# One gate block of a filtered feed-forward layer moved from VectorE to ScalarE and GpSimd, and the order of the sums around it

## The chip, the cores and the metric

The kernel runs on one core of a Trainium2 chip. A core has five engines with a queue of their own each: TensorE (PE, matrix products; its weight loads are shown as PEld), VectorE (DVE), ScalarE (ACT), GpSimd (POOL) and SyncE (SP, which here issues the DMAs). Each queue runs in the order in which it was written, and an instruction that waits holds up everything behind it on its engine. The metric is the device time of one execution in microseconds (us), the median over several runs.

## The reference

Four layers follow each other on an image x of 2 batches, 64 channels and 256 x 256 points, each of the form x = x + layer(group_norm(x)). Layer 0 is a weighted sum over neighbours, layer 1 two state-space scans over the points, layer 3 a rounded cosine transform. The change is in layer 2:

```python
def _L2_conv_ref(x, w_in, w_dw, fft_filter, w_out):
    x = jnp.einsum('bchw,oc->bohw', x, w_in)          # 64 -> 384 channels
    B, C, H, W = x.shape
    xp = x.reshape(B, C, H // p, p, W // p, p).transpose(0, 1, 2, 4, 3, 5)
    xf = jnp.fft.rfft2(xp) * fft_filter               # on patches of 8 x 8
    xp = jnp.fft.irfft2(xf, s=(p, p))
    x = xp.transpose(0, 1, 2, 4, 3, 5).reshape(B, C, H, W)
    x = lax.conv_general_dilated(x, w_dw, window_strides=(1, 1),
            padding=[(1, 1), (1, 1)], feature_group_count=C)   # 3 x 3, by channel
    x1, x2 = jnp.split(x, 2, axis=1)                  # 192 gates, 192 values
    x = jax.nn.gelu(x1, approximate=False) * x2
    return jnp.einsum('bchw,oc->bohw', x, w_out)      # 192 -> 64 channels
```

So each point of 192 channels needs nine multiply-adds for its gate, nine for its value, a gelu of the gate and a product of the two.

## The kernel before

**Tiles.** All data is float32. The 2 x 64 channels of the input stand on 128 partitions. The 384 hidden channels of two batches are six blocks of 128 partitions: gates a0 and a1 (128 channels of batch 0 and of batch 1), a2 (the other 64 of both batches), and values b0, b1, b2 in the same way. The image is worked in 32 strips of 8 rows. A strip's six blocks lie in three tiles `z[s, p]` (two blocks each, 10 rows with the two rows kept from the strip before). The 3 x 3 filter works on halves of four rows, h = 0 and 1; the projection on quarters of two rows, e = 0 and 1.

**The front stage** makes a strip's z. For one tile of patches t: `norm` (ACT, L191, into xn2), `turn` (four transposes on PE, L897, into the PSUM bank po2, copied to xT by ACT, L899), `fourier` (products with the Fourier basis, L905, again into po2, copied to xf, L907). Then for each of its four groups `hidden` makes two products f (L915, two PSUM banks), `scaled` multiplies them with the filter on VectorE into gf (L922), and `image` brings them back to the image (L941, two PSUM banks pz), from where ACT copies them into z (L949).

**The filter stage** of a strip, with each block's 3 x 3 taps done by one of three means:
- on TensorE (`gate_pe`): nine products with a diagonal matrix, L1064, summed in the single PSUM bank pcv; ACT then takes the gelu into the tile gl (L1072). Blocks (h, a0) of both halves.
- on ACT and GpSimd (`gate_pool`): ACT makes the product with one tap (L1017, the first into gl, the others into one of three buffers `prod`), GpSimd adds it to gl (L1021), two rows at a time; the gelu is put off until the third tap of the next piece (`flush`, L995). Blocks (0, a1), (1, a2), (1, a1).
- on VectorE (`taps_of`): the first tap L977, eight more L980, in the PSUM tile acc (two banks, one buffer). `gate_dve` does so for the gate block (0, a2), with the last tap into gl and a gelu behind it; `value_dve` for all six value blocks, with the product of gate and value behind it (L1049).

**The end.** `project` makes the output of two rows (L1093, L1100) in po2, `finish` adds it to the input xr (L1111), takes the statistics for the next norm (L1112) and stores it. po2 has one buffer, which `turn`, `fourier` and `project` share: each has to wait until the one before was read.

**The order** is written out by hand (`tc.manual_schedule`): instructions stand on each engine in the order in which the program issues them, and the waits follow from the tiles. The loop runs over u, half a tile of the front stage; strip s is filtered nine steps later, v = u - 9, in eight steps of two parts g. I call these 16 parts of a strip its slots, i = 0 to 15 (slot i is step j = i // 2, part g = i % 2). A slot issues: the f of `hidden`, two of VectorE's list `dve`, the gf of `scaled`, the rest of VectorE's share (`quota` spreads the list evenly over 16 slots), a projection if one is due, then in an inner loop images, tap products of TensorE's list `pe` and steps of GpSimd's list `gps`, and then `finish` and `turn`. Outputs are due in slots 2 and 5 (the strip before, half 1) and in 10 and 13 (half 0). The boundary rows of the next strip (`edges`, GpSimd, L957 and L959) are copied in slot 14.

```python
dve = gate_dve(s, 0, 2)
for h in range(2):
    for i in ((2, 1, 0), (2, 0, 1))[h]:
        dve += value_dve(s, h, i)
```

Of the kernel before, what the change touches and what calls it, by code (L numbers as in the profile page):

```python
# [10 lines left out]
F32 = mybir.dt.float32  # L11
BF16 = mybir.dt.bfloat16
AF = mybir.ActivationFunctionType
ALU = mybir.AluOpType
# [3 lines left out]
P = 128  # L18
# [102 lines left out]
class Kernel:  # L121
# [695 lines left out]
    def layer2(self, x, y, coeffs):  # L817
        nc, tc, a = self.nc, self.tc, self.a
# [14 lines left out]
        nstrip = H // 8  # L833
        with ExitStack() as ctx:
# [47 lines left out]
                x_half[n] = t  # L882

            def norm(t):
                xn = pool.tile([P, 4, P], F32, name="xn2")
                at = slice(64 * (t % 2), 64 * (t % 2) + 64)
                self.affine(
                    xn.rearrange("p g (i c) -> p i g c", c=16),
                    x_half[t // 2][:, :, at].rearrange("p i (g c) -> p i g c", c=16),
                    coeffs,  # L890
                )
                x_n[t] = xn
# [9 lines left out]
            def fourier(t):  # L902
                pf = p_o.tile([P, 4, P], F32, name="po2")
                for g in range(4):
                    nc.tensor.matmul(pf[:, g], x_T[t][:, g], fwd, start=True, stop=True)  # L905
                xf = pool.tile([P, 4, P], F32, name="xf")
                nc.scalar.copy(xf, pf)  # L907
                x_f[t] = xf
# [75 lines left out]
                return [lambda k=k: step(k) for k in range(9)], box  # L984

            def new_gl(s, h, i, r):
                t = pool.tile([P, 4, W], F32, name="gl", bufs=6)
                gl[s, h, i] = t
                return t[:, :r]

            def new_acc(r):
                return p_a.tile([P, 4, W], F32, name="acc")[:, :r]
# [10 lines left out]
            def gate_pool(s, h, i, r=4):  # L1003

                name, out = f"a{i}", []

                def step(m, n, k):
                    if k == 2:
                        flush()
                    w = taps[name][:, k : k + 1]  # L1010
                    if m == k == 0:
                        new_gl(s, h, i, r)
                    acc = gl[s, h, i][:, m : m + n]
                    prod = acc
                    if k:
                        prod = pool.tile([P, 2, W], F32, name="prod", bufs=3)[:, :n]
                    nc.scalar.activation(  # L1017
                        prod, near(s, name, 4 * h + m, n, k), AF.Copy, scale=w
                    )
                    if k:  # L1020
                        nc.gpsimd.tensor_add(acc, acc, prod)  # L1021
                    if k == 8:
                        late.append(acc)

                for m in range(0, r, 2):
                    for k in range(9):
                        out.append(lambda m=m, k=k: step(m, min(2, r - m), k))
                return out

            def gate_dve(s, h, i, r=4):  # L1030
                ops, box = taps_of(
                    nc.vector,
                    s,
                    f"a{i}",
                    4 * h,
                    r,
                    lambda: new_acc(r),
                    lambda t: new_gl(s, h, i, r),
                )
                return ops[:8] + [lambda: (ops[8](), gelu(gl[s, h, i][:, :r]))]  # L1040

            def value_dve(s, h, i, r=4):
                ops, box = taps_of(
                    nc.vector, s, f"b{i}", 4 * h, r, lambda: new_acc(r), lambda t: t
                )

                def gate():
                    t = gl[s, h, i][:, :r]
                    nc.vector.tensor_tensor(t, t, box["t"], ALU.mult)  # L1049

                return ops + [gate]

            def gate_pe(s, h, i, r=4):
                out = []
# [61 lines left out]
            def quota(n, i, parts):  # L1116
                return n * (i + 1) // parts - n * i // parts

            E = mybir.EngineType
            with tc.manual_schedule(engines={E.PE, E.DVE, E.Activation, E.Pool, E.SP}):  # L1120
                frame(0)
                edges(0)
                load_half(0)
                load_half(1)
                norm(0)
                turn(0)
                fourier(0)
                n_u = 8 * nstrip
                dve, pe, gps = [], [], []
                for u in range(n_u + 12):  # L1130
                    t, odd = divmod(u, 2)
                    front = u < n_u
                    v = u - 9
                    s, j = divmod(v, 8)
                    if j == 0 and 0 <= s < nstrip:
                        dve = gate_dve(s, 0, 2)
                        for h in range(2):
                            for i in ((2, 1, 0), (2, 0, 1))[h]:
                                dve += value_dve(s, h, i)
                        pe = gate_pe(s, 0, 0) + gate_pe(s, 1, 0)  # L1140
                        gps = gate_pool(s, 0, 1) + gate_pool(s, 1, 2) + gate_pool(s, 1, 1)
                        n_dve, n_gps = len(dve), len(gps)
                    if front:
                        if u % 4 == 2 and u // 4 + 2 < 2 * nstrip:
                            load_half(u // 4 + 2)
                        if not odd and t + 1 < 4 * nstrip:
                            norm(t + 1)
                    if u % 8 == 1 and 0 < u - 1 < n_u:
                        frame(u // 8)

                    out = None
                    if 0 <= v:
                        hv, part = divmod(v - 4, 4)
                        if 0 <= hv < 2 * nstrip and part in (0, 1):
                            reload(*divmod(hv, 2), part)
                        hv, part = divmod(v - 5, 4)
                        if 0 <= hv < 2 * nstrip and part in (0, 1):
                            out = (*divmod(hv, 2), part)
                    for g in range(2):
                        i = 2 * j + g  # L1160
                        left = quota(n_dve, i, 16) if 0 <= v and dve else 0
                        if front:
                            ph = hidden(t, 2 * odd + g)
                        for _ in range(min(2, left)):
                            dve.pop(0)()
                        if front:
                            scaled(t, 2 * odd + g, ph)
                        for _ in range(left - min(2, left)):
                            dve.pop(0)()
                        if out and g == odd:  # L1170
                            po = project(*out)
                        images = ((0, 1), (2,))[g] if 0 < u <= n_u else ()
                        n_pe = min(3, len(pe))
                        for n in range(3):
                            if n < len(images):
                                image(u - 1, images[n])
                            if n < n_pe:
                                pe.pop(0)()
                            if i < 14 and 0 <= v and gps:
                                for _ in range(quota(n_gps, 3 * i + n, 42)):  # L1180
                                    gps.pop(0)()
                            if n == 1 and g == 0 and odd and front and t + 1 < 4 * nstrip:
                                fourier(t + 1)
                        if i == 14:
                            flush()
                            if 0 <= s < nstrip:
                                if s + 1 == nstrip:
                                    frame(nstrip)
                                edges(s + 1)
                        if out and g == 1:  # L1190
                            finish(*out, po)
                        if g == 1 and not odd and front and t + 1 < 4 * nstrip:
                            turn(t + 1)


                assert not (dve or pe or gps)
                s = nstrip
                reload(s, 0, 0)
                for op in gate_pool(s, 0, 1, 1) + gate_pe(s, 0, 0, 1) + gate_dve(s, 0, 2, 1):
                    op()  # L1200
                flush()
                for i in (2, 1, 0):
                    for op in value_dve(s, 0, i, 1):
                        op()
                finish(s, 0, 0, project(s, 0, 0))
# [109 lines left out]
```

## Time and profile before

| What | us |
|---|---|
| median of 3 runs (lowest, highest) | 19872.43 (19870.87, 19875.25) |
| the profiled execution, its own time | 19870.25 |
| its span, first to last instruction | 19868.5 |
| busy in the span: VectorE | 18868.2 (95%) |
| busy in the span: GpSimd | 15933.1 (80%) |
| busy in the span: TensorE | 14671.3 (74%) |
| busy in the span: ScalarE | 11805.5 (59%) |

The profile is of one execution. The busy shares are means over layers with different limits, so that what a change in layer 2 does has to be read from layer 2's part of the span. In a row of groups the columns are line, engine, operation, output and inputs with their shapes, count, busy time, mean ns of one, and the idle time of the engine just before them with what ended it. In a row of waits, "A <- B: x, n, m" says that A stood idle for x us in total until B, n times, m at most. A row of a stretch of time has the busy time of each engine in it and TensorE's granted share of its clock.

### The profile page before, as it was taken

To read this page: it belongs to the slowest core of one execution; us is meant where nothing else is said; L and a number is where in the kernel's file an instruction comes from. 1 tells how busy PE (TensorE), PEld (TensorE's weight loads), DVE (VectorE), ACT (ScalarE), POOL (GpSimd) and SP (SyncE) were. 2 spreads that over 40 slices of the span, in tenths; PEclk is the share of its full clock that TensorE was granted. 3 is DMA by queue.
4 is the path that set the end of the run, shared out by engine and by line. 5 is a ranking of instruction groups with operands and counts; after the bars stand their busy time and mean duration, and the time that the engine had idled before them with its cause. 6 is when DMAs were issued, how large, how long until landed. Compare 5 with 4: busy or idle time off the path is not lost. (4 is left out here: it accounts for less than half of the span.)

```text
span 19868.5 us, 162340 instructions
## 1 busy us (share of the span) xinstructions
PE 14671.3 (74%) x48720; PEld 4849.2 (24%) x48720; DVE 18868.2 (95%) x16476; ACT 11805.5 (59%) x16810; POOL 15933.1 (80%) x7816
## 2 busy tenths in 40 slices
PE   6886777677767767677677767677777688888886
PEld 3332111111111111111111111111111144444444
DVE  7998999999999999999999999999999989999997
ACT  1224666666666666666666666666666655555554
POOL 4776888888888888888888888888888855555554
PEclk9997666666666666666666666666666689989998
DMA  3114666666666666666666666666666500000003
GB/s 118 47 46 110 152 152 153 151 154 150 155 148 157 147 157 147 157 148 156 149 154 151 153 152 153 152 153 151 152 151 152 136 29 29 29 29 29 29 27 144
DMA packets 662179, 2438.82 MB, mean 123 GB/s; under 512 B 131888, under 2 KB 201264, under 8 KB 450160
## 3 DMA queue, kind: packets, MB, share of 16 engines
q1 hardware_dynamic: 661296, 2428.43, 50.9%
q8 instruction: 385, 6.31, 0.1%
q14 instruction: 498, 4.08, 0.1%
HBM read 1990.14 MB, written 437.78 MB: 122 GB/s over the span
## 5 line engine op out<-in xcount | busy, mean ns | idle before, releaser
L792 DVE TENSOR_TENSOR_SCAN h<-da,st,h 128x512 f32<-128x512 f32 x8192 | 9837.4, 1262 | 309.0 <-ACT da L789 223.8
L796 POOL TENSOR_TENSOR h<-h,cb 128x2048 f32<-128x2048 f32 x2048 | 9255.6, 4519 | 166.0 <-POOL st L795 1.5
L789 ACT ACTIVATE da<-dl,p_a 128x512 f32<-128x512 f32 x8192 | 5564.8, 688 | 3985.3 <-DVE h L792 3892.6
L561 PE MATMUL py<-h,t_c_quad 128*32 128x512 f32 x16384 | 3254.7, 817 | 1656.9 <-POOL h L796 1655.9
L561 PE MATMUL pb<-bc,t_c_sel 64*128 64x512 f32 x3072 | 2696.9, 972 | 2379.9 <-DVE h L773 2374.3
L773 DVE TENSOR_TENSOR h<-dv,pb 128x2048 f32<-128x2048 f32 x1536 | 3470.5, 2259 | 40.2 <-DMA dv<-d_dv 40.2
L1021 POOL TENSOR_TENSOR gl<-gl,prod 128x512 f32<-128x512 f32 x1544 | 1961.1, 1271 | 1493.3 <-ACT prod L1017 1417.9
L755 POOL TENSOR_TENSOR h<-dv,cb 128x2048 f32<-128x2048 f32 x512 | 2319.8, 4531 | 16.3 <-DMA dl<-d_dl 16.3
L980 DVE SCALAR_TENSOR_TENSOR acc<-z,tap_b,acc 128x1024 f32<-128x1024 f32 (+1 forms) x1560 | 1987.3, 1274 | 38.8
L561 PEld LDWEIGHTS pb<-bc,t_c_sel 64*128 64x128 f32 x3072 | 661.0, 267 | 4406.4 <-DVE h L773 4339.5
L795 POOL COPY st<-h 128x4 f32<-128x4 f32 x2048 | 387.3, 189 | 1360.1 <-DVE h L792 1329.1
L561 PEld LDWEIGHTS py<-h,t_c_quad 128*32 128x32 f32 x16384 | 423.8, 122 | 3821.8 <-POOL h L796 3225.7
L561 PE MATMUL mm<-xin,p_conv 64*128 64x512 f32 x4096 | 1321.1, 774 | 15.4 <-DMA x1t<-y 15.4
L1064 PE MATMUL pcv<-z,diag 128*128 128x512 f32 x2322 | 1172.0, 622 | 20.4 <-ACT gl L1072 16.6
L1017 ACT ACTIVATE prod<-z,tap_a 128x512 f32<-128x512 f32 x1544 | 1045.0, 714 | 37.6 <-POOL gl L1021 37.4
L949 ACT COPY z<-pz 128x512 f32<-128x512 f32 x768 | 456.8, 599 | 1027.3 <-PE pz L941 924.8
L941 PE MATMUL pz<-t_c_inv,gf 128*128 128x128 f32 (+1 forms) x8192 | 1038.5, 309 | 1.4 <-ACT z L949 1.0
L941 PEld LDWEIGHTS pz<-t_c_inv,gf 128*128 128x128 f32 (+1 forms) x8192 | 848.3, 181 | 517.4 <-issue 311.9
L561 PE MATMUL mm<-u,p_dt 128*128 128x512 f32 x1024 | 931.3, 1064 | 0.0
L561 PE MATMUL py<-u,p_d 128*128 128x512 f32 x1024 | 820.9, 895 | 0.0
L915 PE MATMUL f<-t_w_inT,xf 64*128 64x384 f32 x2048 | 597.0, 615 | 156.4 <-DVE gf L922 155.5
L561 PEld LDWEIGHTS mm<-xin,p_conv 64*128 64x128 f32 x4096 | 459.7, 244 | 982.5 <-issue 982.3
(166 smaller groups left out, 17767.8 us busy)
## 6 DMA issues: line engine op xcount, KB each, us to landing
cb<-d_bc SPq DMA_DIRECT2D x2048, 320.0 KB
dl<-d_dl SPq DMA_DIRECT2D x2048, 256.0 KB
dv<-d_dv SPq DMA_DIRECT2D x2048, 256.0 KB
d_dl<-delta SPq DMA_DIRECT2D x256, 512.0 KB
d_dv<-du SPq DMA_DIRECT2D x256, 512.0 KB
xin<-in_x SPq DMA_DIRECT2D x16, 2048.0 KB
xt<-in_x SPq DMA_DIRECT2D x32, 1024.0 KB
y<-yt SPq DMA_DIRECT2D x128, 256.0 KB
```

Of the source, the lines that this page charges most:

```text
L561: nc.tensor.matmul(out, lhsT, rhs, start=start, stop=stop)
L755: nc.gpsimd.tensor_tensor(h, t["dv", b], t["cb", b][:, 0].unsqueeze(1).to_broadcast([P, 4, T]), ALU.mult,)
L773: nc.vector.tensor_tensor(h, t["dv", b], pb.unsqueeze(1).to_broadcast([P, 4, T]), ALU.mult)
L789: nc.scalar.activation(da, t["dl", b][:, k], AF.Exp, scale=ws[m]["a"][:, k, j : j + 1])
L792: nc.vector.tensor_tensor_scan(h[:, k], da, h[:, k], state[m, b][:, j, k : k + 1], ALU.mult, ALU.add)
L796: nc.gpsimd.tensor_tensor(h, h, t["cb", b][:, 1 + j].unsqueeze(1).to_broadcast([P, 4, T]), ALU.mult)
L915: nc.tensor.matmul(p, x_f[t][half, g], w_in[half], start=True, stop=True)
L941: nc.tensor.matmul(pz[i * n : (i + 1) * n, k, :, 16 * g : 16 * g + 16], gf[t, 2 * e + g, b][:, c0 : c0 + n], inv, start=True, stop=True,)
L980: eng.scalar_tensor_tensor(out, near(s, name, m0, r, k), w, box["t"], ALU.mult, ALU.add)
L1017: nc.scalar.activation(prod, near(s, name, 4 * h + m, n, k), AF.Copy, scale=w)
L1021: nc.gpsimd.tensor_add(acc, acc, prod)
L1064: nc.tensor.matmul(box["t"], diag[:, k], near(s, f"a{i}", 4 * h + m, n, k), start=k == 0, stop=k == 8,)
```

## The change

In each strip the gate block (0, a2) leaves VectorE's list. It is made by `gate_pool` now, as the first of four blocks in GpSimd's list. Its value block is the new `value_late`: nine taps on VectorE, the last of which writes into a tile of its own, and the product with the gate is one instruction of GpSimd, issued in slot 5. The other value blocks of a strip are reordered: (0, 0), (0, 1), (1, 0), (1, 2), (1, 1). The ring of gl tiles has seven buffers for six, since the late value takes one, and xn2 has one for two.

In a slot, the inner loop has four parts for three: TensorE's tap products come four to a slot, until the list is empty, and GpSimd's 72 steps are spread over 56 parts of 14 slots, where there were 54 over 42. The rest of VectorE's share is issued behind that loop. In the slots in which an output of an even step is due (3 and 11), `finish` stands right behind the gf of `scaled`, ahead of the rest of VectorE's share, and no longer at the end of the slot; in odd steps (5 and 13) it stays at the end. The single rows behind the last strip are done as before.

```diff
             def norm(t):
-                xn = pool.tile([P, 4, P], F32, name="xn2")
+                xn = pool.tile([P, 4, P], F32, name="xn2", bufs=1)
...
-                t = pool.tile([P, 4, W], F32, name="gl", bufs=6)
+                t = pool.tile([P, 4, W], F32, name="gl", bufs=7)
...
+            def value_late(s, h, i):
+
+                t = pool.tile([P, 4, W], F32, name="gl", bufs=7)
+                ops, _ = taps_of(
+                    nc.vector, s, f"b{i}", 4 * h, 4, lambda: new_acc(4), lambda _: t
+                )
+                return ops, lambda: nc.gpsimd.tensor_tensor(
+                    gl[s, h, i], gl[s, h, i], t, ALU.mult
+                )
...
-                        dve = gate_dve(s, 0, 2)
-                        for h in range(2):
-                            for i in ((2, 1, 0), (2, 0, 1))[h]:
-                                dve += value_dve(s, h, i)
+                        dve, gate_late = value_late(s, 0, 2)
+                        for h, i in ((0, 0), (0, 1), (1, 0), (1, 2), (1, 1)):
+                            dve += value_dve(s, h, i)
                         pe = gate_pe(s, 0, 0) + gate_pe(s, 1, 0)
-                        gps = gate_pool(s, 0, 1) + gate_pool(s, 1, 2) + gate_pool(s, 1, 1)
+                        gps = []
+                        for h, i in ((0, 2), (0, 1), (1, 2), (1, 1)):
+                            gps += gate_pool(s, h, i)
...
                         if front:
                             scaled(t, 2 * odd + g, ph)
-                        for _ in range(left - min(2, left)):
-                            dve.pop(0)()
+                        if out and g == 1 and not odd:
+                            finish(*out, po)
                         if out and g == odd:
                             po = project(*out)
                         images = ((0, 1), (2,))[g] if 0 < u <= n_u else ()
-                        n_pe = min(3, len(pe))
-                        for n in range(3):
+                        n_pe = min(4, len(pe))
+                        if i == 5 and 0 <= s < nstrip:
+                            gate_late()
+                        for n in range(4):
...
-                                for _ in range(quota(n_gps, 3 * i + n, 42)):
+                                for _ in range(quota(n_gps, 4 * i + n, 56)):
                                     gps.pop(0)()
...
+                        for _ in range(left - min(2, left)):
+                            dve.pop(0)()
                         if i == 14:
                             flush()
...
-                        if out and g == 1:
+                        if out and g == 1 and odd:
                             finish(*out, po)
```

## The prediction

> **What bounds the kernel now.** The change touches layer 2 alone, so I first look in the page's slices for its stretch. The 40 slices are 496.7 us each; layer 2 runs from about 15,940 us (first gf) to 19,545 us (last sum), the eight columns before the last one.
>
> ```profile
> DVE  7998999999999999999999999999999989999997
> POOL 4776888888888888888888888888888855555554
> PEclk9997666666666666666666666666666689989998
> ```
>
> VectorE is full there (9), GpSimd half full (5), TensorE's clock about nine tenths. Next, the stretch of one strip, from its first tap on VectorE (17,214.22 us) to the next strip's (17,324.38), and two short stretches in which TensorE had just been idle:
>
> ```profile
> 17214.22:17324.38 110.16, 97.66 (x479) 53.60 (x480) 106.64 (x110) 62.84 (x103) 64.44 (x54) 0.93 0.09 29
> 17240.60:17244.00 3.40, 3.40 (x12) 1.99 (x12) 3.30 (x4) 0.59 (x1) 1.28 (x2) 0.51 0.21 77
> ```
>
> The columns are PE, PE loads, DVE, ACT, POOL busy, then the clock. A strip takes 110.16 us, and VectorE works 106.64 of them; the rest is the 0.03 to 0.04 us between one tap and the next, which depends on it. ACT (62.8) and POOL (64.4) have room. Then the groups of this strip, and who waited:
>
> ```profile
> L980 DVE SCALAR_TENSOR_TENSOR acc<-z,tap_a,acc 128x1024 f32<-128x1024 f32 x7 | 9.0, 1287 | 0.2
> L1021 POOL TENSOR_TENSOR gl<-gl,prod 128x512 f32<-128x512 f32 x48 | 61.1, 1274 | 45.2 <-ACT prod L1017 42.8
> L1049 DVE TENSOR_TENSOR gl<-gl,acc 128x1024 f32<-128x1024 f32 x6 | 7.3, 1219 | 0.5
> ...
> POOL gl L1021 <- ACT prod L1017: 42.8, 18, 12.4
> PE po L897 <- DVE xr L1111: 7.4, 2, 4.1
> PE f L915 <- DVE gf L922: 4.8, 3, 3.4
> ```
>
> VectorE hardly waits (0.8 us, for f); POOL waits 45 us of the strip for products; TensorE waits for VectorE: twice for the sum (xr) that frees the bank of po2. So VectorE's queue sets the strip's time. Last, TensorE's timeline, where it runs without a gap:
>
> ```profile
> 17334.90 1.08 PE L1093 MATMUL po<-gl,w_full 128*64 128x512 f32 x4
> 17335.91 1.12 PE L1100 MATMUL po<-gl,w_both 128*128 128x512 f32 x2
> 17336.87 1.20 PE L941 MATMUL pz<-t_c_inv,gf 128*128 128x128 f32 x12
> 17337.99 1.13 PE L1064 MATMUL pcv<-z,diag 128*128 128x512 f32 x2
> 17338.96 1.19 PE L941 MATMUL pz<-t_c_inv,gf 128*128 128x128 f32 x12
> 17340.08 1.99 PE L1064 MATMUL pcv<-z,diag 128*128 128x512 f32 x4
> 17342.00 0.92 PE L915 MATMUL f<-t_w_inT,xf 64*128 64x384 f32 x4
> 17342.84 1.16 PE L941 MATMUL pz<-t_c_inv,gf 128*128 128x128 f32 x8
> 17343.84 2.74 PE L1064 MATMUL pcv<-z,diag 128*128 128x512 f32 x6
> ```
>
> Start to start gives what each really costs: f pair 0.84, image of six products 1.12 and of four 1.00, one tap product 0.97, two 1.92, projection 1.97. I need these below.
>
> **What the Trainium skill says.** "Trainium Kernel Development and Optimization", Performance Expectations: matmul busy time is a bad metric, as matmuls are pipelined. It agrees here: one image is 1.19 busy but 1.12 apart, so I count starts and not the 97.66. "TensorE: Matmul & The Clock Gate", Part 1: after an idle window of some 3.4 us the clock halves until TensorE has been busy for about as long. The second windows line agrees: 0.51 in the 3.4 us behind a 3.27 us wait. "GPSIMD Engine Reference", section 1: GpSimd contends with VectorE only where that runs a 2-port mode or reads two SBUF inputs. VectorE's taps and gates have one tensor input in PSUM (except the first tap, which has one input in all); the trace's POOL sums agree, 1274 ns median, 1291 at most. So I price POOL's new work as the old.
>
> **The change, part by part.** A strip has 16 slots (u's two halves).
>
> *VectorE loses* gate block a2 of half 0: nine taps, 1.325 us start to start (seven in 9.24 us in the timeline), 11.9 us; and one product with the gate (1.22, with its gap 1.3), which GpSimd takes. 13.2 of 110.16: 97.0 us a strip if nothing else stops it. The last value tap writes to gl rather than acc, same shape: 1.28 either way in the trace (tap into gl, 1281 ns).
>
> *POOL gains* 16 sums: 64 instead of 48. Eight in a row took 10.80 us, so 1.36 apart: 86.9. The new product is 128x1024; between 1.274 (128x512) and the 4.518 of a 128x2048 product in layer 1 (L796) I get 2.36, with its gap 2.4. Its bounds are 1.3 and 4.5. The edge copies and memsets took 3.6 (17,312.75 to 17,316.32). Sum 92.9 of a strip, where it was 69: hidden only while VectorE or TensorE takes longer.
>
> *ACT gains* 18 products at 0.715 and two gelus of 0.63 for one of 1.06: 62.8 + 13.1 = 76. Room remains, but it is in order: its copies of images (z from pz) stand behind products that wait for one of three prod buffers, and each gelu waits for POOL's ninth tap. If POOL is late, ACT is, then the images, then f, then VectorE.
>
> *TensorE* has the same work, but 4 tap products a slot in slots 0 to 8 where it had 3 in slots 0 to 11. Worked from the starts above: a half-slot with two images is f 0.84 + 2.24 + 0.97 + 2.67 = 6.7, with the turned tile's transform (0.89, and one break more between tap products) 7.8; one with one image 0.84 + 1.00 + 3.5 = 5.3. Slots 0 to 8: three of 7.8, two of 6.7, four of 5.3, two projections 3.9, two transposes at some 0.6 each (half of the 1.04 at half clock): 63 us. VectorE's queue over the same stretch, from one slot-15 gf to the gf of slot 9, has 37 tap or gate instructions at 1.315, nine gf pairs at 0.87 and two sums with statistics at 1.4: 59.3. TensorE's f of slot 9 comes 0.85 + 63.5 = 64.4 after the start. So TensorE, ahead of VectorE by some 4 us at first, falls behind by 5.1 and VectorE waits that long in slots 5, 7 and 9. In slots 9 to 15 TensorE has 24 us of work and VectorE 37: VectorE leads again, and the lost 5 us stay lost. Bounds: 1 us (if tap products overlap better) to 10 (if TensorE starts the strip at half clock, 3.4 us at double price, or waits for ACT's gelu before the single pcv bank is free).
>
> *The sum right behind gf* (slots 3 and 11) comes two VectorE instructions or so (about 2.6 us) earlier: VectorE executes the same, no cost; the bank po2 and the transposes behind it are freed earlier, TensorE's 3.3 to 4.1 us waits shrink. Without it TensorE's list above would have another 2 to 3 us. The store follows on SP sooner, where nothing waits.
>
> *Taps moved behind the images in the program, reordered value blocks, gl 7 for 6 buffers, xn2 1 for 2*: VectorE's queue doesn't change by the first. Gates must be there in time: POOL's block (0,1) has 32 sums (43.5), the product (2.4) and a start some 3 us into the strip, with switches of accumulator about 51; VectorE wants it as its 29th instruction, at 47.5 without, 52 to 54 with TensorE's waits. So it is covered by these, just; without them VectorE would wait 3 us there. xn2 is written in slot 2 and its transposes are in slot 3, four slots per round: cover of two slots (12 us). gl has seven allocations a strip, so each waits for its own like of the strip before: free.
>
> *Sum*: 97.0 + 5.1 = 102.1 a strip, 8.06 less, for the 31 strips that still have a front stage. The last strip has none: VectorE took 96.2 there (19,414.8 to 19,511.0), and POOL's 92.9 with its start takes as long: zero, bounds -3 and +6. 31 x 8.06 = 250. The profiled execution took 19870.25 us (span 19868.5), 2 under the median 19872.43: 19872 - 250 = 19622, rounded to **19620 us**. Changes of 0.2% (40 us) are about what a measurement of this kernel can tell.
>
> **Rivals.**
> A (the forecast): TensorE sets slots 2 to 9, 102.1 a strip. For it: the sum of starts above, and that VectorE in the old kernel already waited 0.8 to 1.9 us for f once a strip, in slot 5. Against: the tap products' 3.5 for four is extrapolated from three.
> B: VectorE stays the bound, about 97.3 a strip: 31 x 12.9 = 400, 19470. For it: TensorE's earlier transposes; against: 63 us of products in 59.
> C: POOL sets the strip. 92.9 is its bare work; in slots 0 to 8 it is fed at TensorE's pace, and the trace shows 0.58 to 1.29 us lost at many of its starts behind a k=0 tile. With 13 us of such waits: 106, 31 x 4.2 = 129, 19740.
> D, slower: POOL's lateness closes the ring POOL, ACT's images, TensorE's f, VectorE's gf, POOL's next products. In the old trace POOL waits 45 us a strip; most of it is lack of work, but if more than 17.3 us (110.2 - 92.9) remain, the kernel is slower. With 21 us, 114 a strip: 31 x 3.8 = +118, 19990. Against: three prod buffers (4 us) and two pz banks (a slot) are between.
> That the change doesn't take place is excluded: the built programs' order shows nine taps fewer a strip on VectorE and 16 sums and a product more on GpSimd.
>
> **How the numbers follow.** A 0.52, B 0.17, C 0.21, D 0.08, no difference 0.02. A's own range, from TensorE's waits of 2 to 8 us, is 19530 to 19715. For 8 in 10 the range takes in most of B and C: 19460 to 19790. Faster: A, B and nearly all of C, 0.88; same 0.03; slower 0.09.
>
> **What would show it.** VectorE's taps with tap_a shrink to the last row's 128x256 ones; a strip takes 102 us; VectorE's idle time before gf, released by f, rises from 0.8 to some 5 us a strip, in slots 5, 7, 9; POOL's sums x64 a strip with waits near 8 us; TensorE's waits for xr shorter. Wrong: VectorE idle before L1049 or before a strip's first tap, released by gelu or POOL's edges, means C or D; a strip of 97 us means B.

## The result, and the profile after

The changed kernel takes 19735.52 us (median of six runs, 19733.07 to 19739.94), the kernel before, beside it, 19873.76 (19870.87 to 19876.47): a ratio of 0.9931, 95% interval 0.9918 to 0.9943. It is faster by 138 us. The forecast was 19620: the sign was right, and about half of the expected gain came. In the slices of the page layer 2 begins at the 33rd column (15,940 us / 496.7); it fills seven columns and part of the last, not the "eight columns before the last one" of the prediction:

```profile
DVE  7998999999999999999999999999999978888887
POOL 4776888888888888888888888888888868888885
PEclk9997676666666666666666666666666689999997
```

GpSimd rises from 5 to 8 in layer 2's columns, and VectorE falls from 9 to 8: it now waits. The next two blocks of lines are stretches of the trace after (PE, PE loads, DVE, ACT, POOL busy, then the clock): one strip, from its first tap on, its two halves, and the 3.4 us in which TensorE begins the strip.

```profile
17065.50:17171.00 105.50, 94.62 (x466) 52.32 (x465) 93.22 (x99) 72.95 (x120) 86.90 (x71) 0.94 0.10 31
17065.50:17118.00 52.50, 51.54 (x238) 26.48 (x238) 43.81 (x47) 35.25 (x58) 39.60 (x31) 0.97 0.10 31
17118.00:17171.00 53.00, 43.08 (x230) 25.83 (x229) 49.41 (x53) 37.70 (x63) 47.30 (x41) 0.90 0.10 30
```

```profile
17062.60:17066.00 3.40, 3.34 (x10) 2.04 (x12) 3.19 (x5) 0.00 (x0) 0.46 (x2) 0.50 0.03 5
```

In the first half TensorE has work nearly all the time (51.54 of 52.50) and VectorE hasn't (43.81); in the second it is VectorE that is nearly full (49.41 of 53.00). And TensorE starts the strip at half clock. The groups of that strip, and one row of its waits:

```profile
L1021 POOL TENSOR_TENSOR gl<-gl,prod 128x512 f32<-128x512 f32 x64 | 81.3, 1273 | 19.3 <-ACT prod L1017 15.8
L922 DVE TENSOR_TENSOR gf<-feff,f 128x384 f32<-128x384 f32 x32 | 16.2, 548 | 6.7 <-PE f L915 6.7
L1049 DVE TENSOR_TENSOR gl<-gl,acc 128x1024 f32<-128x1024 f32 x5 | 6.1, 1220 | 3.8 <-ACT gl L995 2.4 <-ACT gl L1082 1.2
L1059 POOL TENSOR_TENSOR gl<-gl 128x1024 f32<-128x1024 f32 x1 | 2.4, 2374 | 0.0
...
PE po L897 <- DVE xr L1121: 4.2, 1, 4.2
```

VectorE's idle time went from 0.8 us for f to 6.7 for f and 3.6 for gates. TensorE's wait for the sum is left once a strip, where it was twice.

A strip's time below is the distance of slot 0's first gf from strip to strip, the mean of strips 3 to 28: 110.15 us before, 105.81 after. 31 x 4.34 = 134.5 us, and the profiled spans (19868.5 and 19734.4) differ by 134.1, so nothing is left for the last strip. Over the stretch from 16,200 to 19,000 us (2800 / 105.81 = 26.5 strips) VectorE's queue waits for, before and then after:

```profile
DVE gf L922 <- PE f L915: 27.4, 25, 2.3
```

```profile
DVE gf L922 <- PE f L915: 162.4, 105, 3.3
DVE gl L1049 <- ACT gl L995: 62.0, 26, 2.4
DVE gl L1049 <- ACT gl L1082: 30.8, 26, 1.2
```

By strip that is 1.1 us before; after, 6.1, 2.3 and 1.2, together 9.6 us. By slot (each wait is put to the gf or the product before which it stands), as means over strips 4 to 25: f 0.65 in slot 1, 1.89 in slot 3, 0.34 in slot 5, 3.25 in slot 7; the gate (0, a0), which ACT takes out of pcv (L1082), 1.19 at the end of slot 4; the gate (0, a1) of ACT and GpSimd (L995) 2.38 in slot 7. VectorE without its waits is 105.8 - 9.6 = 96.2, what the forecast's 97.0 with its 0.8 of old waits says. So the whole miss lies in the waits: 9.6 us, where the forecast had 5.1 and those 0.8.

The half clock at the strip's start also holds back GpSimd, whose first sum needs a product that ACT makes behind the copy of TensorE's first image:

```profile
17064.70 2.27 PE L941 MATMUL pz<-t_c_inv,gf 128*128 128x128 f32 x12
17065.70 1.29 DVE L977 TENSOR_SCALAR acc<-z,tap_b 128x1024 f32<-128x1024 f32 x1
17071.17 1.27 POOL L1021 TENSOR_TENSOR gl<-gl,prod 128x512 f32<-128x512 f32 x1 [8.06 <-ACT prod L1017]
```

Slot 7 in the timeline of the kernel after (start, duration, engine; in brackets the idle time before, and what ended it; rows between are left out):

```profile
17113.87 0.58 ACT L949 COPY z<-pz 128x512 f32<-128x512 f32 x1
17114.35 0.71 ACT L1017 ACTIVATE prod<-z,tap_a 128x512 f32<-128x512 f32 x1
17114.97 0.58 ACT L1082 ACTIVATE gl<-pcv 128x512 f32<-128x512 f32 x1
...
17115.60 1.13 PE L1074 MATMUL pcv<-z,diag 128*128 128x512 f32 x2 [0.96 <-ACT gl L1082]
...
17116.66 0.92 PE L915 MATMUL f<-t_w_inT,xf 64*128 64x384 f32 x4
...
17117.61 1.02 DVE L922 TENSOR_TENSOR gf<-feff,f 128x384 f32<-128x384 f32 x2 [3.26 <-PE f L915]
...
17121.54 0.63 ACT L995 ACTIVATE gl<-gl 128x512 f32<-128x512 f32 x1 [1.01 <-POOL gl L1021]
...
17122.20 1.22 DVE L1049 TENSOR_TENSOR gl<-gl,acc 128x1024 f32<-128x1024 f32 x1 [2.38 <-ACT gl L995]
```

ACT frees pcv only behind an image's copy and a product that stand ahead of the gelu in its queue; TensorE loses 0.96 us there and its f comes late; and one tap later VectorE is stopped again, by the gate (0, a1). The question for the runs: which of these sets the strip, TensorE's list (rival A's mechanism), GpSimd's sums (C's), or both by turns?

### The profile page after: what moved, and what is told of

Read it like the earlier page. It is cut to its first block, busy times and chain, and to the rows that moved or that the text cites. A ratio compares the mean times of both kernels' runs of the same rounds, so it can differ in the third digit from the quotient of the medians.

```text
span 19734.4 us, 163589 instructions
## 1 busy us (share of the span) xinstructions
PE 14596.0 (74%) x48720; PEld 4825.9 (24%) x48720; DVE 18476.6 (94%) x16156; ACT 12171.1 (62%) x17418; POOL 16646.8 (84%) x8360
## 5 line engine op out<-in xcount | busy, mean ns | idle before, releaser
L1021 POOL TENSOR_TENSOR gl<-gl,prod 128x512 f32<-128x512 f32 x2056 | 2606.7, 1271 | 659.0 <-ACT prod L1017 545.4
L980 DVE SCALAR_TENSOR_TENSOR acc<-z,tap_b,acc 128x1024 f32<-128x1024 f32 (+1 forms) x1528 | 1947.0, 1274 | 37.7
L1017 ACT ACTIVATE prod<-z,tap_a 128x512 f32<-128x512 f32 x2056 | 1410.6, 715 | 201.4 <-POOL gl L1021 199.0
L561 PE MATMUL mm<-xin,p_conv 64*128 64x512 f32 x4096 | 1322.2, 774 | 15.8 <-ACT xin L191 15.8
L922 DVE TENSOR_TENSOR gf<-feff,f 128x384 f32<-128x384 f32 x1024 | 519.2, 548 | 240.3 <-PE f L915 240.3
```

The costliest lines, as they stand in the source:

```text
L561: nc.tensor.matmul(out, lhsT, rhs, start=start, stop=stop)
L922: nc.vector.tensor_tensor(o, feff, ph[b], ALU.mult)
L980: eng.scalar_tensor_tensor(out, near(s, name, m0, r, k), w, box["t"], ALU.mult, ALU.add)
L1017: nc.scalar.activation(prod, near(s, name, 4 * h + m, n, k), AF.Copy, scale=w)
```

## The experiments

Every kernel was timed beside the kernel before, in four groups; the kernel before had medians of 19867.8 to 19874.0 us in them, so a few us between runs of different groups say nothing. The intervals of the ratios reach some 30 us to either side. Where I compare two edited kernels by less than that, the claim rests on executions that don't overlap and on the strip times of one trace each. Edits are to the kernel after, but for one. First the sum of all: strip times, VectorE's waits of a strip (all rows of its list of waits from 16,200 to 19,000 us, divided by 2800 us / strip; for the kernel without half of TensorE's taps from the means by slot), and the difference of the two.

| Kernel | median us | strip | VectorE's waits | difference |
|---|---|---|---|---|
| before | 19873.8 | 110.15 | 1.1 | 109.1 |
| after | 19735.5 | 105.81 | 9.6 | 96.2 |
| half of TensorE's taps left out | 19663.8 | 103.1 | 7.2 | 95.9 |
| 14 of GpSimd's sums left out | 19734.4 | 105.81 | 9.6 | 96.2 |
| TensorE's taps spread | 19736.7 | 105.83 | 9.6 | 96.2 |
| late product in slot 8 | 19716.6 | 105.68 | 9.5 | 96.2 |
| GpSimd's blocks swapped | 19733.1 | 105.76 | 9.5 | 96.3 |
| both lists swapped, taps spread | 19767.2 | 107.0 | 10.2 | 96.8 |
| sum at the end again | 19761.7 | 106.68 | 10.7 | 96.0 |
| idle TensorE filled | 19683.7 | 104.1 | 8.2 | 95.9 |
| swapped and spread | 19668.3 | 103.9 | 7.7 | 96.2 |
| swapped, spread and filled | 19682.5 | 104.2 | 8.0 | 96.2 |
| two late values | 19578.7 | 100.7 | 4.4 | 96.3 |

VectorE's own work, 109.1 us in the kernel before, is the same 96 to 97 in all the others. What the edits change is when TensorE's f and the gates arrive.

**Half of TensorE's taps left out.** The test of A: less work on TensorE.

```diff
                     def step(k, m=m, n=n, box=box):
+                        if 3 <= k <= 7:
+                            return
```

> The changed kernel with TensorE's tap products 3 to 7 of each gate piece left out (20 of 36 a strip, some 17 us of TensorE; the output is not the layer's). A strip of the changed kernel takes 105.8 us, with 6.1 us of VectorE's waits for f, 1.2 for the gelu of block (0, a0) and 2.4 for that of (0, a1). T1, TensorE's queue sets the strip: the 7.3 us go and the 2.4 stay, 98.5 a strip, 19510. T2, GpSimd's chain up to the gate (0, a1) sets it and TensorE's waits lie in its shadow: the wait before the product of gate and value in slot 7 grows to 5 to 9 us, 103 to 105.5 a strip, 19650 to 19725.

Measured: 19663.84 us, ratio 0.9894 (0.9879 to 0.9909), 72 us under the kernel after. 20 of 36 tap products at 0.97 us are 19 us of TensorE's time a strip; the strip shrinks by 2.7. VectorE still waits 4.66 us for f in slot 7, and 5.6 in all, where it was 6.1. So neither reading that was named holds: f's waits didn't go, and the gate (0, a1) is waited for less (1.4 us), not more. What TensorE itself waits for, in the kernel after and then here (same stretch of time):

```profile
PE pcv L1074 <- ACT gl L1082: 24.8, 26, 1.0
```

```profile
PE pcv L1076 <- ACT gl L1084: 208.1, 77, 5.3
```

0.9 us a strip became 208.1 / 27.2 = 7.7: relieved of its taps, TensorE stands before the single pcv bank until ACT's gelu has read it. The clock is another part of it: by the records of the two traces TensorE is at half clock for 25.2 us of a strip here, for 14.6 in the kernel after, so part of the time that the edit took from TensorE went into slower products. TensorE's load sets part of the strip at most; the next chain, through ACT's queue, is close behind.

**14 of GpSimd's 64 sums left out.** The test of C.

```diff
-                    if k:
+                    if k and not (h == 0 and i == 2 and k > 1 and r == 4):
                         nc.gpsimd.tensor_add(acc, acc, prod)
```

> The changed kernel with 14 of GpSimd's 64 sums a strip left out (block (0, a2) keeps two taps; ScalarE still makes all products; the output is not the layer's). GpSimd has 19 us less before the gate (0, a1). T1: only the 2.4 us before that gate's product go, TensorE's 7.3 stay: 103.4 a strip, 19661. T2 says the same of the 2.4, but the 7.3 of TensorE then set the strip: also about 103.4. If ScalarE, held up by GpSimd, is what makes TensorE late (T3), the waits for f shrink too: 97 to 100 a strip, 19460 to 19560.

Measured: 19734.39 us, 0.9929 (0.9914 to 0.9944), no difference from the kernel after, though 103.4 a strip was expected by either of the first two readings; every wait of VectorE by slot is the same within 0.05 us. GpSimd's own list of waits, after and then here:

```profile
POOL gl L1021 <- ACT prod L1017: 406.9, 343, 8.2
```

```profile
POOL gl L1021 <- ACT prod L1017: 908.2, 315, 12.7
```

501 us more in 26.5 strips is 18.9 a strip, which is 14 x 1.35: all the time taken from GpSimd became waiting for ACT's products. The gate (0, a1), though its last step is a sum of GpSimd, isn't late because GpSimd is full, at least not by these sums ahead of it: its gelu comes behind the sixth of seven sums in a row, and this row begins at 17113.50 after a wait of 0.53 us for a product of ACT in the kernel after, and in this kernel likewise (17113.26, 0.83 us). ACT issues in order, behind image copies that wait for TensorE (2.95 us before the copy at 17105.17 of the kernel after) and behind gelus that wait for GpSimd (2.09 us before the one at 17110.31).

**TensorE's taps spread.** Four a slot up to slot 5, then three: takes one product out of each of slots 6 to 8.

```diff
-                        n_pe = min(4, len(pe))
+                        n_pe = min(4 if i < 6 else 3, len(pe))
```

> The changed kernel with four tap products a slot on TensorE in slots 0 to 5 only and three after, so that slot 6 holds one less (and the wait for the gelu of the single bank pcv moves behind f of slot 7). T1: the 3.3 us that VectorE waits for f in slot 7 go, 102.5 a strip, 19635. T2: they come back as a longer wait for the gate (0, a1) in the same slot, 2.4 to 5.6 us, and a strip stays at 105.5 to 106, 19730.

Measured: 19736.7 us, 0.9931 (0.9916 to 0.9946): nothing. VectorE's waits here:

```profile
DVE gl L1049 <- ACT gl L995: 116.9, 26, 4.5
DVE gf L922 <- PE f L915: 106.8, 104, 1.9
```

f improves by 2.1 us a strip (162.4 to 106.8) and the gate (0, a1) worsens by 2.1 (62.0 to 116.9). Slot 7's f is 1.17 us late instead of 3.25, and the gate 4.5 instead of 2.4: VectorE only reaches the gate earlier. What was won at f is lost at the gate.

**The late product in slot 8** instead of 5, which takes 2.4 us of GpSimd's work from in front of the gate (0, a1).

```diff
-                        if i == 5 and 0 <= s < nstrip:
+                        if i == 8 and 0 <= s < nstrip:
                             gate_late()
```

> The changed kernel with GpSimd's product of the late value in slot 8 rather than 5, behind the sums of block (0, a1), whose gate comes 2.4 us sooner. T1 and T2: the 2.4 us that VectorE waits for that gate in slot 7 go and TensorE's waits stay, 103.4 a strip, 19661. If the product's place doesn't matter because ScalarE is late with the products anyway (T3), under 1 us a strip, 19705 or more.

Measured: 19716.59 us (19714 to 19728), 0.992 (0.9904 to 0.9937), 19 us under the kernel after. The gate's wait fell from 2.38 to 1.55 and slot 7's f from 3.25 to 2.98, 1.1 us in all, but f in slot 1 rose by 0.94, from 0.65 to 1.59. Only 0.1 us a strip stayed in the execution that was traced; it was the longest of the four (19728, the others 19714 to 19719), so that some more may have stayed in those. I come back to this in the last section.

**GpSimd's blocks swapped**, (0, 1) before (0, 2), with the product in slot 8: the gate (0, a1) has 16 sums less ahead of it.

```diff
-                        for h, i in ((0, 2), (0, 1), (1, 2), (1, 1)):
+                        for h, i in ((0, 1), (0, 2), (1, 2), (1, 1)):
```

> The changed kernel with the first two blocks of GpSimd's list exchanged, (0, a1) before (0, a2), and the late value's product in slot 8. The gate (0, a1) is then ready some 20 us before VectorE asks, and the wait of 2.4 us in slot 7 goes. T1 and T2: TensorE's 7.3 us stay, 103.4 a strip, 19661. If GpSimd's lead also frees ScalarE (T3), less.

Measured: 19733.07 us, 0.9929 (0.9915 to 0.9944): nothing again, by the opposite exchange. The gate's wait is gone from the list, and f has taken its place:

```profile
DVE gf L922 <- PE f L915: 219.7, 132, 3.0
DVE gl L1049 <- ACT gl L1082: 30.9, 26, 1.2
```

219.7 against 162.4 is 2.2 us a strip more, in slot 1 (1.78, where it was 0.65) and slot 9 (1.42, where there was none). Slot 9 is TensorE's chain, reached earlier; slot 1 is the clock at the strip's start (last section). With the run of the spread taps this shows that freeing f or the gate alone gives nothing here.

**Both lists swapped.** Also VectorE's value block (0, 1) before (0, 0), and TensorE's products three in even slots and four in odd ones.

```diff
-                        for h, i in ((0, 0), (0, 1), (1, 0), (1, 2), (1, 1)):
+                        for h, i in ((0, 1), (0, 0), (1, 0), (1, 2), (1, 1)):
...
-                        n_pe = min(4, len(pe))
+                        n_pe = min(3 + g, len(pe))
```

> As the run with GpSimd's blocks exchanged, and with TensorE's tap products spread, three in slots with two images and four in slots with one, and VectorE's first two whole value blocks exchanged, (0, 1) before (0, 0), so that the gate of TensorE is asked for two slots later. T1: VectorE's waits for f fall from 6.1 to 1 or 2 us, that for (0, a0) goes, one of 0 to 2 for (0, a1) in slot 5 may come: 98 to 100.5 a strip, 19495 to 19575. T2 or T3, GpSimd or ScalarE behind it set the strip elsewhere: above 102, 19620.

Measured: 19767.23 us, 0.9947 (0.9932 to 0.9962), 32 us slower than the kernel after. A miss: fewer products a slot bring TensorE's second gate, (1, a0), later, and VectorE now waits for that in slot 10, 3.77 us a strip:

```profile
DVE gl L1049 <- ACT gl L1082: 98.0, 26, 3.8
```

**Swapped and spread.** GpSimd's blocks swapped, product in slot 8, and the taps spread, VectorE's order left: the two edits that gave nothing, together.

```diff
-                        for h, i in ((0, 2), (0, 1), (1, 2), (1, 1)):
+                        for h, i in ((0, 1), (0, 2), (1, 2), (1, 1)):
...
-                        n_pe = min(4, len(pe))
-                        if i == 5 and 0 <= s < nstrip:
+                        n_pe = min(4 if i < 6 else 3, len(pe))
+                        if i == 8 and 0 <= s < nstrip:
```

> The changed kernel with GpSimd's first two blocks exchanged, the late product in slot 8, and four tap products a slot up to slot 5 and three after: neither of the two waits that took each other's place in the single edits can now do so. T4: the half clock at the strip's start still costs its 3 us, and the strip settles where the window boundary lets it, either at 31 windows of 3.413 us (105.8, 19733) or at 30 (102.4, 19628). Without any tie to the windows: 105.8 less the 2.5 to 3.5 us of f in slots 7 and 9, 102.5 to 103.5.

Measured: 19668.26 us (19655 to 19673), 0.9898 (0.9883 to 0.9913): 67 us under the kernel after. The wait for gate (0, a1) is gone, without the one for f in slot 9 that the swap alone had brought; slot 7's f is 1.17 late. What else is left is mainly f in slots 1 and 3 (1.09, 1.89) and the gates of TensorE, (0, a0) 1.19 and (1, a0) 1.78.

**Idle TensorE filled.** Twelve products of TensorE a strip in slots 11 to 15, whose result nothing reads, in the kernel after. They are there only to keep its clock up.

```diff
+            def filler(s):
+                t = p_c.tile([P, 2, W], F32, name="pcv")
+                nc.tensor.matmul(
+                    t, diag[:, 0], near(s, "a0", 0, 2, 0), start=True, stop=True
+                )
...
+                        if front and 0 <= s:
+                            for _ in range({11: 4, 12: 1, 13: 2, 14: 2, 15: 3}.get(i, 0)):
+                                filler(s)
```

> The changed kernel with 12 tap products a strip more on TensorE, whose results nothing reads (4 in slot 11, 1 in 12, 2, 2 and 3 in slots 13 to 15), in places where TensorE waits for VectorE. They keep it busy, so that its clock doesn't fall. T4: the strip is bound by the clock's return at a window boundary some 1.3 us behind the gf of slot 0; with TensorE at full clock f and the images of slots 0 and 1 come some 3 us sooner, and everything behind them: 102.5 to 103.5 a strip, 19635 to 19665. T1, the sum of TensorE's products alone: no gain, or slower by what the 12 products delay f in slots 12 to 0, 105.8 to 107, 19735 to 19775.

Measured: 19683.68 us, 0.9907 (0.9891 to 0.9924): 52 us under the kernel after (46 if each is taken against the kernel before of its own group), with more work. The place of the strip's start that was shown at 0.50 above, here:

```profile
17045.70:17049.10 3.40, 3.40 (x23) 1.95 (x22) 3.19 (x5) 0.99 (x2) 0.52 (x2) 1.00 0.00 0
```

Full clock, and 23 matmuls where there were 10. TensorE's timeline of the same place, after and then here:

```profile
17062.66 2.11 PE L915 MATMUL f<-t_w_inT,xf 64*128 64x384 f32 x4 [2.11 <-DVE gf L922]
17064.70 2.27 PE L941 MATMUL pz<-t_c_inv,gf 128*128 128x128 f32 x12
17066.90 1.86 PE L1074 MATMUL pcv<-z,diag 128*128 128x512 f32 x2
```

```profile
17046.43 0.92 PE L915 MATMUL f<-t_w_inT,xf 64*128 64x384 f32 x4
17047.28 1.30 PE L941 MATMUL pz<-t_c_inv,gf 128*128 128x128 f32 x12
17048.51 1.13 PE L1080 MATMUL pcv<-z,diag 128*128 128x512 f32 x2
```

In the kernel after these three take 5.94 us from start to start of what follows, here 3.04. f's waits in slots 1 and 3 fall by 0.65 and 0.96; all others stay, though VectorE gets to them sooner, because GpSimd's chain starts sooner too: its first sum comes 0.7 us behind slot 0's gf, the mean of strips 3 to 28, where it was 2.4. So the half clock costs the kernel after 1.7 us a strip (105.81 to 104.1).

**Swapped, spread and filled**: the last two together, so, on top of the swapped and spread kernel, with the same `filler`:

```diff
+                        if front and 0 <= s:
+                            for _ in range({11: 4, 12: 1, 13: 2, 14: 2, 15: 3}.get(i, 0)):
+                                filler(s)
```

> As the run with the blocks exchanged and the products spread, with the 12 idle tap products. T4: both the waits for f in slots 7 and 9 and the half clock at the start are gone: 99 to 101 a strip, 19525 to 19590. T1, no effect of the clock: as without the idle products, or slower.

Measured: 19682.48 us, 0.9906 (0.9892 to 0.9921): 14 us worse than without the filling. A miss. The unread products now stand in front of f in slots in which TensorE is no longer early enough: VectorE waits for f in slot 13, 1.5 us in every other strip or 0.78 on average, where it was 0.04. And though TensorE is at full clock at every strip's start, f is still 0.87 and 1.89 us late in slots 1 and 3: full clock helps only where TensorE has the time to come first.

**The sum at the end again**, in the kernel after.

```diff
-                        if out and g == 1 and not odd:
-                            finish(*out, po)
...
-                        if out and g == 1 and odd:
+                        if out and g == 1:
                             finish(*out, po)
```

> The changed kernel with the sum with the projection back at the end of the slot. The forecast's step: TensorE's transposes of slot 3 wait some 2.6 us longer for the bank, f of slot 4 with them, 2 to 3 us a strip: 19797 to 19828. If this wait lies in the shadow of GpSimd's gate (T2): under 0.7 us a strip, 19735 to 19757.

Measured: 19761.71 us, 0.9944 (0.9927 to 0.996), 26 us over the kernel after, 0.87 a strip. TensorE's wait for xr grows from 4.1 to 6.7 us a strip, after and then here:

```profile
PE po L897 <- DVE xr L1121: 109.8, 26, 4.2
```

```profile
PE po L897 <- DVE xr L1121: 175.2, 26, 6.7
```

**The early sum alone, in the kernel before.** The same edit the other way round.

```diff
+                        if out and g == 1 and not odd:
+                            finish(*out, po)
...
-                        if out and g == 1:
+                        if out and g == 1 and odd:
                             finish(*out, po)
```

> The kernel before with this one part of the change, the sum with the projection right behind gf in slots 3 and 11. VectorE does the same work and waits 1.1 us a strip for f in slot 5, behind the late transposes; only this can be won: 31 times 1.1 is 35, 19838. If it delays VectorE elsewhere: 19873 or more.

Measured: 19845.04 us, 0.9986 (0.9979 to 0.9993), 29 us won. TensorE's waits for the sum, before and then here:

```profile
PE po L897 <- DVE xr L1111: 191.8, 50, 4.2
```

```profile
PE po L897 <- DVE xr L1111: 3.6, 11, 0.3
```

VectorE's 1.1 us for f in slot 5 is gone, and 0.02 us of waits a strip is left on it; a strip takes 109.22 us. That is as much as the kernel before could win by it: VectorE was its bound.

**Two late values.** If f and the gates can't come earlier, VectorE can want them later. A second value block, (1, 2), is filtered before (1, 0) into a tile of its own (one buffer, which both late values share, so that gl needs six); its product follows on VectorE behind (1, 0). The blocks of GpSimd are swapped, VectorE takes (0, 1) before (0, 0), and TensorE's taps are three a slot again.

```diff
-            def value_late(s, h, i):
+            def value_late(s, h, i, eng=nc.gpsimd):
 
-                t = pool.tile([P, 4, W], F32, name="gl", bufs=7)
+                t = pool.tile([P, 4, W], F32, name="late_v", bufs=1)
...
-                        for h, i in ((0, 0), (0, 1), (1, 0), (1, 2), (1, 1)):
+                        for h, i in ((0, 1), (0, 0)):
                             dve += value_dve(s, h, i)
+                        ops, gate_late2 = value_late(s, 1, 2, nc.vector)
+                        dve += ops + value_dve(s, 1, 0) + [gate_late2] + value_dve(s, 1, 1)
...
-                        n_pe = min(4, len(pe))
-                        if i == 5 and 0 <= s < nstrip:
+                        n_pe = min(3, len(pe))
+                        if i == 8 and 0 <= s < nstrip:
```

> The changed kernel with a second late value: (1, 2) is made before (1, 0), its taps end in a tile of their own and its product is taken on VectorE behind (1, 0). Block (1, 0), whose gate TensorE makes, is thus asked for in slot 13 and not in slot 10, and (0, 0) in slot 7, so that TensorE's tap products are spread three a slot over slots 0 to 11 as in the kernel before; GpSimd makes (0, a1) before (0, a2), the late product of (0, 2) is in slot 8. If the forecast's sum over TensorE's slots was the right kind of bound, VectorE's waits for f fall from 6.1 to 1 or 2 us a strip; 98.5 to 101 a strip, 19510 to 19590. If GpSimd's own work with its waits takes over (some 98.4 by its busy time and the waits of the changed kernel that aren't at the strip's start), the waits show before the product of gate and value in slot 5: 101 to 103, 19590 to 19650. If neither: about 104, 19680.

Measured: **19578.73 us** (19576.73 to 19583.0), ratio 0.9852 (0.9835 to 0.9868): 294 us under the kernel before, 157 under the kernel after. VectorE's list of waits has two rows of any size left:

```profile
DVE gf L922 <- PE f L915: 87.3, 61, 2.4
DVE xr L1121 <- PE po L1110: 34.9, 20, 2.2
```

No gate is waited for, f is waited for mainly in slots 11 and 13 (0.80 and 2.23 us), and xr 1.3 us in slot 13. With the same VectorE work and the same TensorE products as in the kernel after, 5.1 us a strip come back. The run has several edits at once, and one more thing goes with them: TensorE's half clock ends 1.4 us or more before slot 0's gf in every strip, and no f is late in slot 1.

## Why the prediction was right or wrong

**VectorE loses 13.2 us a strip**: right. Its own work is 96.2 us where the forecast's 97.0 less 0.8 of old waits gives 96.2; by means over the strips it lost 12.9.

**POOL gains**: right in size and in not being the bound. The product took 2.374 us against the 2.36 interpolated. GpSimd is busy 86.9 us a strip; that the forecast has the same number for the sums alone is chance, as it counted from start to start (1.36 for a sum of 1.27), 92.9 in all. Its waits are 15.8 us, not near 8, and they are for ACT's products. Rival C's number, 19740, is almost the time measured, and C's mark, VectorE idle before L1049, was there. C's mechanism, that GpSimd's own work sets the strip, wasn't: 19 us less of sums moved nothing. A time that agrees with a rival's doesn't make the rival right.

**TensorE, 63 us of products against VectorE's 59**: right in that VectorE waits for f, wrong in part in what makes f late, and near in size by luck. The term was 5.1 us in slots 5, 7 and 9 (the list of slots adds up to 63.1, and 63.5 was carried on, a slip of 0.4). It measures 6.1: 2.5 in slots 1 and 3, 0.3 in slot 5, 3.3 in slot 7 and none in 9. Load has a share in slot 7, since one product less in each of slots 6 to 8 took 2.1 us off it. But with 20 of 36 taps left out f's waits only fell to 5.6, so that the sum of products alone doesn't set them. Two things that the step had put into its upper bound, and not into the 5.1, happened: the strip starts at half clock (f, image and tap pair 2.9 us longer than at full clock, of which 1.7 reach the end, shown by filling), and TensorE waits for ACT's gelu before pcv is free (0.96 us in slot 7). The same single bank and ACT's in-order queue make the gate (0, a0) late by a further 1.2 us, for which the sum had no term. The working took TensorE to be ahead by some 4 us at first; at the half clock it isn't.

**Gates must be there in time**: this step failed. "Covered by these, just" assumed that TensorE's waits give the gate (0, a1) the time it needs. They don't: 2.4 us are missing, and 4.5 when f comes earlier. VectorE was there 54.1 us into the strip shown, as forecast ("52 to 54"), but the gate came at 56.5, for "about 51". GpSimd's start was 5.5 us into the strip (first sum at 17071.17, first tap at 17065.70), for "some 3"; on average 1.7 us of that go when TensorE is kept at full clock. From there GpSimd goes at the pace of ACT's products. Summed: 6.1 + 1.2 + 2.3 = 9.6, where the forecast had 5.1 and, inside its 97.0, the old 0.8; 3.7 x 31 = 115 us, which is the whole miss (19735 - 19620).

**The sum right behind gf**: right in direction, too large by two or three times. "Another 2 to 3 us" a strip was 0.87. TensorE's wait does grow by 2.5 us without it, but the wait is in slot 11, in a half of the strip in which TensorE has time to spare (43.08 busy of 53.00 us), so that most of it doesn't reach the end.

**Last strip zero**: right (134.5 us in the 31 strips, 134.1 in the span).

**The range** held the time, since it reached to C. A's own range, 19530 to 19715, didn't: it gave its upper bound to TensorE's waits alone and took the gates as free.

## What to carry to other kernels

When work leaves the bounding engine, list every engine's product that its queue consumes (here f from TensorE, two kinds of gates) with the time at which it is ready and wanted; what ends the gain is the latest of several, and where two are within a few us, an edit to one shows nothing and the pair must be tried together. If the producers can't be quicker, reorder the consumer: the version that put independent taps in front of a late gate, and spread TensorE's taps to fit, came to 157 us under the kernel after with no work removed. And a rival whose time fits is to be tested by its mechanism, by taking the suspected work away and seeing whether the wait moves.

## What the runs showed of the hardware

In most of these runs a strip's time locks to TensorE's clock. "TensorE: Matmul & The Clock Gate", Part 1, of the Trainium skill says that the clock is decided in windows of 4096 cycles, 3413 ns, that run freely. The traces agree: in 21 strips of the kernel after, all 114 changes of the granted clock lie a whole number of 3.413 us apart, to within 0.004. In the run with the late product in slot 8 and in the swapped one nearly all strips take 105.81 us, which is 31 x 3.413, with TensorE at half clock from 8.9 us before to 1.3 us behind slot 0's gf in each such strip. In the kernel after, strips take 105.51, 105.55 and 106.38 in turn, 317.4 = 93 x 3.413; with the sum at the end again four take 426.7 = 125 windows, with two late values four take 402.8 = 118, and the early sum in the old kernel gave 109.21 in nearly every strip, 32 windows (109.2). With its idle time filled, the kernel has no half clock in the strips of layer 2 before the last, and takes 104.1.

How late f comes in slot 1 depends on where the half clock ends, once that is behind slot 0's gf. The run with the late product in slot 8 shows it from strip to strip, with one and the same program:

| half clock ends, from slot 0's gf on (us) | f late in slot 1 (us) |
|---|---|
| -2.28 | 0.22 |
| -1.30 | 0.51 |
| -0.02 | 0.43 |
| 0.95 | 1.43 |
| 1.31 (most strips) | 1.79 |
| 2.70 | 2.38 |

In the kernel after it ends between -0.7 and +0.2, and the wait is 0.65 on average. So the strip of the late product, which would be shorter by its 1.1 us of slot 7, reaches its start earlier in the window, has more half clock in front of it, and gives 0.94 of that back in slot 1. The swapped kernel gives back 1.1 in the same way. That the locking holds the period where it is, I argue from the periods, as no run shifted the window alone. It doesn't bind every kernel: the swapped and spread one has no such pattern (its strips take 102.5 to 105.3 us), and on top of it the filling won nothing.

What stays open: the 1.19 us before the gate (0, a0), which of the runs with VectorE's order as it was only the one with half of TensorE's taps made smaller (0.1), and how much of the gain of the version with two late values is due to each of its parts.
